# A graph network's edge sweep: edge products in two halves of TensorE, node tiles spread over a block, pass 0's rows through PSUM, and no counting

## The chip, the cores and the metric

The kernel runs on one core of a Trainium2 chip. The metric is the device time of one execution in microseconds (us). Ten executions of the kernel before took 3209.31 to 3219.22 us, with a median of 3214.12 us.

A core has five engines that run their own instruction streams in order and wait for each other by semaphores: TensorE (PE, matrix products, with PEld for its weight loads), VectorE (DVE), ScalarE (ACT), GpSimd (POOL) and SyncE (SP). DMAs are issued from the queues of SP, ACT and POOL. A DMA whose rows are picked by a list of indices (a gather) is issued from POOL, which is busy with it for about a microsecond.

## The reference

The graph has N = 6250 nodes of 256 features and E = 100000 edges, sorted by their target `dst`, with 64 features per edge. There are three message passes:

```
pass 0:  e    = relu((x[dst] - x[src]) @ theta.T + theta_b + x[src] @ phi.T + phi_b)
         out  = segment_max(e, dst), 0 where a node has no edge
         x    = layernorm(x + out)
         hv   = x @ W_in + b_in
pass 1, pass 2 (weights W_u0, then W_u1):
         m    = relu(concat(hv[src], he) @ W + b)
         hv   = hv + segment_max(m, dst) where a node has an edge, else hv
result:  y    = layernorm(x + relu(hv @ W_ro + b_ro))
```

Here `he` are the 64 edge features. All numbers are float32.

## The kernel before

**Tables.** A product with a node's features is the same for all edges that leave it, so each pass has a table in DRAM with one row of 256 numbers per node. An edge's message is its source's table row, plus, in passes 1 and 2, the product of its 64 edge features with the lower part of the weights. Table 0 is made in a prologue; tables 1 and 2 are written tile by tile as node results appear (`first_g` L924 to L928, `next_d` L941 to L944).

**Steps, chunks, blocks.** The edges are laid out in reverse order in 14 blocks. A block has 56 steps (the last 54), FS = 782 in all; step s takes one edge on each of the 128 partitions, and a partition's edges follow each other in a block. Per step GpSimd gathers 128 table rows into `run` (`sources`, L784). Eight steps share one `run` buffer, a chunk; there are four such buffers. The gather for step s + 16 is issued at step s (`AHEAD`). Then VectorE makes the running maximum along each partition: the message of the step before is cut by `lim` (minus a huge number where a new target begins) and compared with the step's row (L1043). Each finished chunk is stored to DRAM as `S` (L1051), on the SP queue. The running value is written over the gathered row, so the first step of a chunk reads the last row of the chunk before.

**Rows of a step.** In pass 0 the row is the gathered one, in SBUF; for 40 of the first 160 steps it is instead made from gathered rows of x (`raw_turn`, `raw_pair`) and lies in PSUM. In passes 1 and 2, `pair` (L816) makes the edge product of two steps at once: the features of the two steps stand one above the other in the 128 rows of the contraction, and the weights `whe` stand twice in a 128 x 512 block with zeros elsewhere. VectorE adds the two gathered rows to it in PSUM (L1030), then does the two steps of the maximum.

**Blocks and nodes.** At the end of a block the running values of the 128 partitions are carried over the lanes (`over_lanes`). The nodes lie in 49 tiles of 128, handled from tile 48 down to tile 0. For a tile, GpSimd gathers from `S` the row where each node's edges end (`rows`, L866, list `end_i`). `picks` and `carried` bring in what was carried from lanes before; then comes the rest of the node's computation, cut into small tasks (`first_a` to `first_g`, `next_a` to `next_d`, `last_d` to `last_g`).

**The order.** It is written out by hand. `at(slot, task)` files a task under a step; the loop over s issues the step's own instructions and then the tasks of that slot. Each engine gets its instructions in this order. A node tile has a base slot b, and a slot g for its gather. In passes 1 and 2 a tile follows the last block that it needs by 20 steps, with a gap of 4 or 6 steps to the tile before. In pass 0 the ends of the nodes' edges must be known first: `count` (L707) makes one-hot matrices from all targets and adds their products on TensorE, three steps apart from step 28 on; `ends_a` and `ends_b` make `has` and `end_i` from the counts. So no tile of pass 0 has a gather before step 324 (`begin`), and tile 48's base is 344.

**From one pass to the next.** The first 24 steps of a pass (`EARLY`) gather only from the part of the table that tiles 1 to 48 wrote. What comes from tile 0 is added on TensorE: a `row` of source numbers is loaded on SP, VectorE makes a 0/1 matrix `own` of it (L824), and TensorE multiplies that with tile 0's result `new0` (L829). Of these 24 gathers, 8 are issued at the last 8 steps of the pass before (`FIRM`) and 16 after the tasks of slot FS:

```
        for f, a in tasks.pop(FS):
            f(*a)
        if r < 2:
            for s in range(FIRM, EARLY):
                sources_next(s)
```

Tile 0 has base FS + 4 = 786 and its gather at slot 782. The later gathers read the whole table and so need tile 0's table write. The edge features of a pass are loaded from ScalarE's queue from the pass's step 0 on (`features`, L811).

Of the kernel before, what the change touches and what calls it, by code (L numbers as in the profile page):

```python
# [17 lines left out]
P = 128  # L18
N = 6250
D = 256  # L20
# [44 lines left out]
WIDE = max(sum(a <= b <= z for a, z in SPAN) for b in range(NB))  # L65

# [7 lines left out]
def gather_raw(nc, x, x_sb, s_r, i):  # L74

    nc.gpsimd.indirect_dma_start(out=x_sb[:, i, :], out_offset=None, in_=x,
                                 in_offset=bass.IndirectOffsetOnAxis(ap=s_r[:, i:i + 1], axis=0))
# [382 lines left out]
def gnn_kernel(  # L460
# [13 lines left out]
    above = const.tile([P, P], F32)  # L474
    nc.vector.tensor_scalar(above, jmp, 0.0, None, OP.is_gt)
# [4 lines left out]
    col = const.tile([P, P], BF16)  # L480
    nc.vector.tensor_copy(col, col_i)
# [30 lines left out]
    lo = const.tile([P, FS], BF16)  # L512
    hi = const.tile([P, FS], BF16)
    with tc.manual_schedule(), tc.tile_pool(name="pro", bufs=2) as pro, \
# [6 lines left out]
        for i in range(SOON):  # L521
            gather_raw(nc, x, x_sb, s_r, i)
        zero = pro.tile([1, D], F32, name="zero", bufs=1)
# [14 lines left out]
        def check():  # L538
# [15 lines left out]
            alike = BLOCKS.count(BLOCKS[0])  # L554
# [9 lines left out]
            nc.vector.tensor_scalar(bits, d_s, P - 1, None, OP.bitwise_and)  # L564
            nc.vector.tensor_copy(lo, bits)
            nc.vector.tensor_scalar(bits, d_s, 7, None, OP.arith_shift_right)
            nc.vector.tensor_copy(hi, bits)
# [29 lines left out]
def in_order(ctx: ExitStack, tc: tile.TileContext, g):  # L597
# [9 lines left out]
    table, ident, above, every, col, col_f = (g[n] for n in ("table", "ident", "above", "every", "col", "col_f"))  # L607
    whole, lim, lo, hi, s_s, fd, pd, ld, nd = (g[n] for n in ("whole", "lim", "lo", "hi", "s_s", "fd", "pd", "ld", "nd"))
    heT, xTn, xn, out = (g[n] for n in ("heT", "xTn", "xn", "out"))
    s_e, head, x, x_sb, wd, s_r = (g[n] for n in ("s_e", "head", "x", "x_sb", "wd", "s_r"))  # L610
    part = g["part"]
# [6 lines left out]
    has = one.tile([P, NT], F32, name="has")  # L618
# [3 lines left out]
    ones = one.tile([P, NT], F32, name="ones")  # L622
    nc.vector.memset(ones, 1.0)
# [30 lines left out]
    for r, w in enumerate((g["w_u0"], g["w_u1"])):  # L654
        t = one.tile([P, 2, D], F32, name=f"whe{r}")
        nc.vector.memset(t, 0.0)
        for s in range(2):
            nc.scalar.dma_start(t[s * DE:(s + 1) * DE, s, :], w[D:, :])
        whe.append(t)
# [36 lines left out]
    hist = psum.tile([P, 512], F32, tag="v", name="hist", bufs=1)  # L696

    none = one.tile([P, NT], BF16, name="none")
    nc.vector.memset(none, 0.0)
    half = (NG + 1) // 2  # L700
    low = []
    for i in range(2):
        low.append(psum.tile([P, 512], F32, tag="he", name="low", bufs=3))
        n = min(half * K, FS - i * half * K)
        nc.scalar.copy(low[i][:, :n], lo[:, i * half * K:i * half * K + n])

    def count(c):  # L707
        k = min(K, FS - c * K)
        ol = work.tile([P, K, P], BF16, name="ol", bufs=1)
        nc.vector.tensor_tensor(ol[:, :k, :], col.unsqueeze(1).to_broadcast([P, k, P]),  # L710
                                low[c // half][:, c % half * K:c % half * K + k].unsqueeze(2).to_broadcast([P, k, P]), OP.is_equal)
        b = max(i for i in range(NB) if FIRST[i] <= c * K)
        tiles = [t for t in range(NT) if SPAN[t][0] <= b <= SPAN[t][1]]
        t0, w = tiles[0], len(tiles)
        oh = work.tile([P, K, WIDE], BF16, name="oh", bufs=1)
        nc.vector.tensor_tensor(oh[:, :k, :w], col[:, t0:t0 + w].unsqueeze(1).to_broadcast([P, k, w]),  # L716
                                hi[:, c * K:c * K + k].unsqueeze(2).to_broadcast([P, k, w]), OP.is_equal)
        if c == 0:
            nc.tensor.matmul(hist[:, :NT], ol[:, 0, :], none, start=True, stop=False)
        for j in range(k):  # L720
            nc.tensor.matmul(hist[:, t0:t0 + w], ol[:, j, :], oh[:, j, :w], start=False,  # L721
                             stop=(c == NG - 1 and j == k - 1))

    cnt, incl, end = (one.tile([P, NT], F32, name=n) for n in ("cnt", "incl", "end"))
    sums = []

    def ends_a():
        nc.vector.tensor_copy(cnt, hist[:, :NT])
        ps = psum.tile([P, 512], F32, tag="pr", name="sums")
        nc.tensor.matmul(ps[:, :NT], above, cnt, start=True, stop=True)  # L730
        nc.tensor.matmul(ps[:, 64:64 + NT], every, cnt, start=True, stop=True)
        sums.append(ps)
        nc.vector.tensor_scalar(has, cnt, 0.0, None, OP.is_gt)

    def ends_b():
        lower, total = sums[0][:, :NT], sums[0][:, 64:64 + NT]
        nc.vector.tensor_tensor_scan(incl, ones, total, 0.0, OP.mult, OP.add)
        nc.vector.tensor_sub(end, total, incl)
        nc.vector.tensor_sub(end, end, lower)
        nc.vector.tensor_add(end, end, has)  # L740
        nc.vector.tensor_scalar(end, end, float(E - 2), 0.0, OP.add, OP.max)
        nc.vector.tensor_copy(end_i, end)
# [14 lines left out]
    def turned(a):  # L757
        tp = psum.tile([P, 512], F32, tag="tp", name="tp")
        for k in range(2):
            nc.tensor.transpose(tp[:, k * P:(k + 1) * P], a[:, k * P:(k + 1) * P], ident)  # L760
        aT = work.tile([P, 2, P], F32, name="aT")
        nc.scalar.copy(aT.rearrange("p k e -> p (k e)"), tp[:, :2 * P])  # L762
        return aT

    def times(aT, w, n, tag="pr"):
        ps = psum.tile([P, 512], F32, tag=tag, name="prod", bufs=3 if tag == "he" else 2)
# [4 lines left out]
    def sweep(r):  # L771
# [7 lines left out]
        carried_in = []  # L779
        pending = []  # L780
# [13 lines left out]
        def raw_turn(i):  # L794

            tp = psum.tile([P, 512], F32, tag="tp", name="tp")
            for q in range(4):
                nc.tensor.transpose(tp[:, q * P:(q + 1) * P], x_sb[:, 2 * i + q // 2, q % 2 * P:(q % 2 + 1) * P], ident)
# [3 lines left out]
        def raw_pair(i):  # L802
            aT = rT.pop(i)
            hp[i * K // 2] = psum.tile([P, 512], F32, tag="pr", name="hp")
            for q in range(4):
                nc.tensor.matmul(hp[i * K // 2][:, q // 2 * D:(q // 2 + 1) * D], aT[:, q, :], wd[:, q % 2, :],
# [9 lines left out]
        def pair(i):  # L816
            c, q = divmod(i, K // 2)
            hp[i] = psum.tile([P, 512], F32, tag="he", name="hp", bufs=3)
            early = 2 * i < EARLY
            if early:  # L820
                row = work.tile([P, 2 * P], I32, name="row")
                nc.sync.dma_start(row, head[i:i + 1, :].to_broadcast([P, 2 * P]))
                own = work.tile([P, 2 * P], F32, name="own")
                nc.vector.tensor_scalar(own, row, part, None, OP.is_equal)  # L824
            nc.tensor.matmul(hp[i], hT[c][:, q, :], whe[r - 1].rearrange("p s f -> p (s f)"), start=True,  # L825
                             stop=not early)
            if early:
# [291 lines left out]
```

## Time and profile before

| what | value |
|---|---|
| median of 10 runs | 3214.12 us |
| profiled execution, its own time | 3213.0 us |
| its span, first to last instruction | 3211.2 us |
| mean granted clock of TensorE | 0.737 |
| HBM read, written | 404.56 MB, 333.17 MB |
| S store, from issue to landing (median) | 4.8 us |
| edge features | 4.4 us |
| table gather | 3.3 us |
| m gather | 2.9 us |
| table write of a tile | 3.6 us |

The profile's page gives for each engine its busy time and share of the span. The costliest groups of instructions show source line, engine, operation, what is written and read, shapes and count; after the bar come the busy time, the mean ns of one, and the engine's idle time just before them with what ended it. "issue" means that the profile shows nothing waited for. In a table by stretches, a row gives the stretch (us from the start), its length, the busy time and number of instructions of the named engine, TensorE's granted clock, the share of time in which DMA engines were busy, and GB/s. A timeline row gives start, duration, engine, line, operation and tiles, how many were merged, and in square brackets the idle time before it and what ended it. An engine's letter with a q (ACTq) is its queue, issuing a DMA.

### The profile page before, as it was taken

How to read it: one execution, taken by the hardware profiler on the slowest of the kernel's cores; microseconds unless marked ns; L12 is line 12 of the kernel's file. 1: busy time of each engine (PE TensorE's matmuls, PEld its weight loads, DVE VectorE, ACT ScalarE, POOL GpSimd, SP SyncE). 2: the span in 40 equal slices, each digit the busy share in tenths (PEclk: the TensorE clock that was granted, in tenths of full speed). 3: DMA queues.
4: the chain of work that ended last, by engine and by line, in shares of the span. 5: the costliest groups of instructions: out<-in, count | busy, mean ns of one | idle time of the engine just before them, and what ended most of it. 6: DMA issues, size and time to landing. Idle time of an engine off the chain costs nothing. (4 is left out here: it accounts for less than half of the span.)

```text
span 3211.2 us, 21650 instructions
## 1 busy us (share of the span) xinstructions
PE 1889.4 (59%) x4631; PEld 849.4 (26%) x4631; DVE 2126.3 (66%) x4750; ACT 238.5 (7%) x618; POOL 2394.6 (75%) x2500
## 2 busy tenths in 40 slices
PE   6663336566511266666666666656666666666665
PEld 5542213222200122232222222223333222222221
DVE  2788756656544376666666666657777777777766
ACT  2000001111100000000000000000001000000000
POOL 6767777777777767777777777776777777777775
PEclk8765556656555588888878877769888888777777
DMA  9769666656666576777667776767767676677775
GB/s 308 242 223 316 220 221 203 206 194 207 206 211 207 194 248 228 233 235 235 228 232 243 236 237 232 235 221 242 241 230 230 233 237 226 234 234 242 236 233 191
DMA packets 241821, 739.39 MB, mean 230 GB/s; under 512 B 52485, under 2 KB 95858, under 8 KB 204434
## 3 DMA queue, kind: packets, MB, share of 16 engines
q0 software_dynamic: 119664, 326.92, 34.1%
q1 hardware_dynamic: 69568, 337.85, 28.3%
q10 hardware_dynamic: 52450, 73.16, 6.8%
q14 instruction: 100, 0.82, 0.1%
q8 instruction: 39, 0.64, 0.1%
HBM read 404.56 MB, written 333.17 MB: 230 GB/s over the span
## 5 line engine op out<-in xcount | busy, mean ns | idle before, releaser
L790 POOL DMA_INDIRECT run<-table,s_s x2258 | 2165.6, 959 | 718.3 <-issue 607.7
L825 PE MATMUL hp<-whe,hT 128*128 128x512 f32 x1564 | 1061.7, 790 | 523.5 <-DVE run L1043 507.3
L1030 DVE TENSOR_TENSOR hp<-hp,run 128x512 f32<-128x512 f32 x782 | 543.8, 695 | 464.1 <-DMA run<-table,s_s 439.3
L1043 DVE SCALAR_TENSOR_TENSOR run<-run,lim,hp 128x256 f32<-128x256 f32 x1573 | 753.7, 479 | 46.8
L825 PEld LDWEIGHTS hp<-whe,hT 128*128 128x128 f32 x1564 | 327.6, 240 | 1079.3 <-DVE run L1043 1021.2
L1043 DVE SCALAR_TENSOR_TENSOR run<-run,lim 128x256 f32<-128x256 f32 x731 | 351.9, 481 | 231.9 <-DMA run<-table,s_s 217.3
L889 PE MATMUL v<-cs,pick 128*128 128x256 f32 (+1 forms) x438 | 167.5, 504 | 140.5 <-DVE pick L882 140.5
L768 PE MATMUL prod<-wcat,aT 128*128 128x512 f32 x196 | 174.6, 1043 | 23.2 <-ACT aT L762 23.2
L870 POOL DMA_INDIRECT m<-S,end_i x147 | 143.5, 976 | 52.7 <-issue 43.2
L889 PEld LDWEIGHTS v<-cs,pick 128*128 128x128 f32 x438 | 104.2, 257 | 253.1 <-issue 147.2
L721 PE MATMUL hist<-oh,ol 128*128 128x8 bf16 (+7 forms) x782 | 34.8, 167 | 177.2 <-DVE oh L716 177.2
L710 DVE TENSOR_TENSOR ol<-col,low 128x1024 bf16<-128x1024 bf16 x98 | 118.7, 1211 | 7.2 <-PE hist L721 7.1
L760 PE MATMUL tp<-ident,h_sb 128*128 128x128 f32 x196 | 49.5, 342 | 120.7 <-DVE h_sb L935 120.2
L932 ACT ACTIVATE m<-m,has 128x256 f32<-128x256 f32 x98 | 49.7, 508 | 697.3 <-DVE m L931 670.1
L840 PE MATMUL lp<-ident,run 128*128 128x128 f32 x84 | 24.9, 393 | 126.0 <-DVE run L1043 117.3
L760 PE MATMUL tp<-ident,x_sb 128*128 128x128 f32 x98 | 31.9, 425 | 110.9 <-DVE x_sb L755 70.8
L768 PE MATMUL prod<-wro,aT 128*128 128x256 f32 x196 | 79.6, 545 | 25.3 <-ACT aT L762 25.3
L721 PEld LDWEIGHTS <-ol 128*128 128x128 bf16 x782 | 36.3, 104 | 202.3 <-DVE ol L710 197.7
L768 PE MATMUL prod<-wt,xT 128*128 128x256 f32 x196 | 88.4, 598 | 0.4 <-DMA xT<-in_xTn 0.4
L762 ACT COPY aT<-tp 128x256 f32<-128x256 f32 x147 | 54.7, 372 | 444.0 <-PE tp L760 421.6
L768 PEld LDWEIGHTS prod<-wcat,aT 128*128 128x128 f32 x196 | 55.9, 313 | 88.7 <-issue 48.1
L760 PEld LDWEIGHTS tp<-ident,h_sb 128*128 128x128 f32 x196 | 23.3, 163 | 210.5 <-issue 123.4
(131 smaller groups left out, 1326.6 us busy)
## 6 DMA issues: line engine op xcount, KB each, us to landing
S<-run SPq DMA_DIRECT2D x291, 1024.0 KB, 4.8
hT<-in_heT ACTq DMA_DIRECT2D x196, 256.0 KB, 4.4
run<-table,s_s POOLq DMA_INDIRECT x2258, 3.3
table<-new ACTq DMA_DIRECT2D x98, 128.0 KB, 3.6
xg<-in_xTn SPq DMA_DIRECT2D x7, 896.0 KB, 9.0
xT<-in_xTn SPq DMA_DIRECT2D x49, 128.0 KB, 5.0
x_sb<-in_xn SPq DMA_DIRECT2D x7, 896.0 KB, 7.5
out<-new ACTq DMA_DIRECT2D x48, 128.0 KB, 2.5
```

The costliest lines, as they stand in the source:

```text
L710: nc.vector.tensor_tensor(ol[:, :k, :], col.unsqueeze(1).to_broadcast([P, k, P]), low[c // half][:, c % half * K:c % half * K + k].unsquee ...
L721: nc.tensor.matmul(hist[:, t0:t0 + w], ol[:, j, :], oh[:, j, :w], start=False, stop=(c == NG - 1 and j == k - 1))
L760: nc.tensor.transpose(tp[:, k * P:(k + 1) * P], a[:, k * P:(k + 1) * P], ident)
L762: nc.scalar.copy(aT.rearrange("p k e -> p (k e)"), tp[:, :2 * P])
L768: nc.tensor.matmul(ps[:, :n], aT[:, k, :], w[:, k, :], start=(k == 0), stop=(k == 1))
L790: nc.gpsimd.indirect_dma_start(out=runs[s // K][:, s % K, :], out_offset=None, in_=table[r][:SPARE + 1, :] if early else table[r], in_offs ...
L825: nc.tensor.matmul(hp[i], hT[c][:, q, :], whe[r - 1].rearrange("p s f -> p (s f)"), start=True, stop=not early)
L870: i = nc.gpsimd.indirect_dma_start(out=o["m"], out_offset=None, in_=S_r[:P * (FIRST[SPAN[t][1]] + BLOCKS[SPAN[t][1]]), :], in_offset=bass. ...
L889: nc.tensor.matmul(o["v"][:, :N1], p, cs[:, blk % KEPT, :N1], start=(blk == SPAN[t][0]), stop=(blk == SPAN[t][1]))
L932: nc.scalar.activation(o["m"], o["m"], AF.Relu, scale=has[:, t:t + 1])
L1030: nc.vector.tensor_add(sums, sums, two)
L1043: nc.vector.scalar_tensor_tensor(cur, prev, lim[:, s:s + 1], row, OP.min, OP.max)
```

## The change

Five things change together.

1. The edge products: `pair` becomes `four`. The 64 features of one step are multiplied with a plain 64 x 256 weight block, in the upper or the lower 64 rows of TensorE according to the step's place, and go to two PSUM tiles, one per half. Four steps are made at once; VectorE's sum covers steps s and s + 2, or s + 1 and s + 3.
2. Pass 0's gathered rows are copied to PSUM by ScalarE, two steps at a time (`bring`), four steps ahead of VectorE, whose maximum then always reads its row from PSUM. The rows from x go into the same PSUM tiles.
3. `count`, `ends_a` and `ends_b` go. A new task `ends` per tile finds where its nodes' edges end by two small masks per block, one product per block with `lane` (each partition's targets, plus one), and two sums on VectorE. `has` becomes `keeps`, a limit of plus or minus a huge number that a minimum applies, so ScalarE's relu with scale in `first_b` and `next_a` is no longer there.
4. Node tiles are spread: the gap is the block's 56 steps divided by its tiles, at least 8; the first base in all three passes is 84, and tile 0's is FS + 6. The theta product stays in PSUM and comes just before its use. The table of x is loaded part by part from step 2 on.
5. PSUM is shared out anew: the tag `he` has four buffers (three before), `tp` one (two before).

The core of the diff:

```diff
+    def ends(t):
+        b0, b1 = SPAN[t]
+        top = work.tile([P, NB], F32, name="top")
+        nc.vector.tensor_scalar(top[:, b0:b1 + 1], fn[:, 0, b0:b1 + 1], float(-P * t), None, OP.add)
+        ps = psum.tile([P, 512], F32, tag="he", name="ends", bufs=4)
+        for b in range(b0, b1 + 1):
+            own = work.tile([P, P], F32, name="here")
+            nc.vector.tensor_scalar(own, col_f, fn[:, 1, b:b + 1], float(-P * t), OP.subtract, OP.is_gt)
+            nc.vector.scalar_tensor_tensor(own, col_f, top[:, b:b + 1], own, OP.is_le, OP.mult)
+            nc.tensor.matmul(ps[:, :BLOCKS[0] + 1], own, lane[:, b, :], start=b == b0, stop=b == b1)
+        found = work.tile([P, 2, BLOCKS[0]], F32, name="found")
+        num = work.tile([P, 2], F32, name="num")
+        for i, op in enumerate((OP.is_ge, OP.is_equal)):
+            nc.vector.scalar_tensor_tensor(found[:, i, :], ps[:, :BLOCKS[0]], n1[:, t:t + 1], every[:, :BLOCKS[0]], op,
+                                           OP.mult, accum_out=num[:, i:i + 1])
+        nc.vector.tensor_scalar(end_i[:, t:t + 1], ps[:, BLOCKS[0]:BLOCKS[0] + 1], num[:, 0:1], 0.0, OP.add, OP.max)
+        nc.vector.tensor_scalar(keeps[:, t:t + 1], num[:, 1:2], 0.0, 2.0 * BIG, OP.is_gt, OP.mult)
+        nc.vector.tensor_scalar(keeps[:, t:t + 1], keeps[:, t:t + 1], -BIG, None, OP.add)
...
+        def bring(i):
+            hp[i] = psum.tile([P, 512], F32, tag="he", name="hp", bufs=4)
+            if raw(2 * i) is None:
+                c, q = divmod(i, K // 2)
+                nc.scalar.copy(hp[i], runs[c][:, 2 * q:2 * q + 2, :].rearrange("p s f -> p (s f)"))
+                return
+            aT = rT.pop(raw(2 * i) // 2)
...
-            nc.tensor.matmul(hp[i], hT[c][:, q, :], whe[r - 1].rearrange("p s f -> p (s f)"), start=True,
-                             stop=not early)
+        def four(u):
+            c, q = divmod(u, K // 4)
+            hp[u] = [psum.tile([P, 512], F32, tag="he", name="hp", bufs=4) for _ in range(2)]
+            early = 4 * u < EARLY
+            n = min(2, FS // 2 - 2 * u)
+            for j in range(n):
+                i = 2 * u + j
+                if early:
+                    row = work.tile([P, 2 * P], I32, name="row")
+                    nc.sync.dma_start(row, head[i:i + 1, :].to_broadcast([P, 2 * P]))
+                    own = work.tile([P, 2 * P], F32, name="own")
+                    nc.vector.tensor_scalar(own, row, part, None, OP.is_equal)
                 for k in range(2):
+                    at_ = slice(k * DE, (k + 1) * DE)
+                    nc.tensor.matmul(hp[u][k][:, j * D:(j + 1) * D], hT[c][at_, 2 * q + j, :], whe[r - 1][at_, :],
+                                     start=True, stop=not early)
+                if early:
+                    for k in range(2):
+                        nc.tensor.matmul(hp[u][k][:, j * D:(j + 1) * D], own[:, k * P:(k + 1) * P], new0, start=False,
+                                         stop=True)
...
-                nc.vector.tensor_add(o["m"], o["m"], h_sb[:, t, :])
-                nc.scalar.activation(o["m"], o["m"], AF.Relu, scale=has[:, t:t + 1])
-
-            def first_c():
-                nc.vector.tensor_add(o["m"], o["m"], x_sb[:, t, :])
+                nc.vector.scalar_tensor_tensor(o["m"], o["m"], keeps[:, t:t + 1], o["h"][:, :D], OP.min, OP.add)
+                nc.vector.scalar_tensor_tensor(o["m"], o["m"], 0.0, x_sb[:, t, :], OP.max, OP.add)
...
-                nc.vector.tensor_max(o["m"], o["m"], o["v"][:, :D])
-                nc.scalar.activation(o["m"], o["m"], AF.Relu, scale=has[:, t:t + 1])
+                nc.vector.scalar_tensor_tensor(o["m"], o["m"], keeps[:, t:t + 1], o["v"][:, :D], OP.min, OP.max)
...
-        gap = (6, 4, 6)[r]
+        last = [FIRST[b] + BLOCKS[b] for _, b in SPAN]
         b = 0
         for t in reversed(range(NT)):
-            e = max(FIRST[SPAN[t][1]] + BLOCKS[SPAN[t][1]], begin)
-            b = max(b + (gap if b < FS else 3), e + 4, min(e + AHEAD + 4, FS + 4))
-            node(t, max(e, b - AHEAD - 4), b)
+            e = last[t]
+            gap = max(8, BLOCKS[0] // last.count(e))
+            b = max(b + gap, e + AHEAD + 12)
+            b = min(b, FS - FIRM - 12 - 8 * (t - 1)) if t else FS + 6
+            node(t, max(min(e + 8, b - 4), b - AHEAD - 4), b)
...
+            if r > 0:
+                if s % 4 == 0 and s + 4 < FS:
+                    four(s // 4 + 1)
+                sums = hp[s // 4][s % 2]
+                if s % 4 < 2:
+                    n = min(2, (FS - s + 1) // 2)
+                    sums = sums.rearrange("p (a f) -> p a f", f=D)[:, :n, :]
+                    nc.vector.tensor_add(sums, sums, runs[c][:, j:j + 2 * n - 1:2, :])
+                row = hp[s // 4][s % 2][:, s % 4 // 2 * D:(s % 4 // 2 + 1) * D]
```

## The prediction

> **What bounds the kernel now.** I read the busy times first, then gather counts by stretch, then the timelines of GpSimd, VectorE, ScalarE and TensorE where one pass hands over to the next.
>
> ```profile
> PE 1889.4 (59%) x4631; PEld 849.4 (26%) x4631; DVE 2126.3 (66%) x4750; ACT 238.5 (7%) x618; POOL 2394.6 (75%) x2500
> ...
> L790 POOL DMA_INDIRECT run<-table,s_s x2258 | 2165.6, 959 | 718.3 <-issue 607.7
> L825 PE MATMUL hp<-whe,hT 128*128 128x512 f32 x1564 | 1061.7, 790 | 523.5 <-DVE run L1043 507.3
> ...
> L1043 DVE SCALAR_TENSOR_TENSOR run<-run,lim 128x256 f32<-128x256 f32 x731 | 351.9, 481 | 231.9 <-DMA run<-table,s_s 217.3
> ```
>
> GpSimd is 75% busy, and nearly all its idle time ends by "issue": 0.30 us between one gather and the next. A gather costs 0.95 + 0.30 = 1.25 us, and there are 2493 of them (2258 + 48 + 147 + 40): 2493 x 1.25 = 3116 of the 3211.2 us. The other engines wait: TensorE idles 523.5 us ahead of its largest group. So only what shortens a gather, or makes GpSimd wait, counts. The number of gathers does not change.
>
> Gathers by stretch (us, GpSimd busy, count):
>
> ```profile
> 80.00:160.00 80.00, 60.49 (x63) 0.75 0.74 244
> 160.00:240.00 80.00, 54.04 (x57) 0.67 0.67 220
> 240.00:480.00 240.00, 183.03 (x188) 0.50 0.76 252
> 480.00:880.00 400.00, 306.72 (x307) 0.62 0.62 204
> 880.00:1090.00 210.00, 159.51 (x165) 0.53 0.61 207
> ...
> 1200.00:2080.00 880.00, 666.15 (x703) 0.81 0.71 234
> 2240.00:3120.00 880.00, 666.27 (x702) 0.80 0.70 235
> ```
>
> Passes 1 and 2 do 1405 gathers in 1760 us, 1.2527 each. Pass 0 does 780 in 1010 us; at 1.2527 that is 977.1, so pass 0 loses 32.9 us. In the timeline of 80 to 240 us, 9.6 us of it are idle gaps above 0.30 (2.76, 2.22, 2.02 and smaller), where VectorE is late while it counts. The other 23.3 are longer gathers (306.72/307 = 1.00 us, against 666.15/703 = 0.948).
>
> GpSimd at the change from pass 0 to 1:
>
> ```profile
> 1096.27 0.95 POOL L790 DMA_INDIRECT run<-table,s_e  x1 [0.30 <-issue]
> 1097.52 0.95 POOL L870 DMA_INDIRECT m<-S,end_i  x1 [0.30 <-issue]
> 1098.78 0.95 POOL L790 DMA_INDIRECT run<-table,s_e  x1 [0.30 <-issue]
> ...
> 1127.56 0.95 POOL L790 DMA_INDIRECT run<-table,s_s  x1 [0.30 <-issue]
> 1135.62 0.94 POOL L790 DMA_INDIRECT run<-table,s_s  x1 [7.11 <-DVE run L1043]
> ```
>
> VectorE over the same stretch, then ScalarE and TensorE:
>
> ```profile
> 1100.33 0.48 DVE L905 SCALAR_TENSOR_TENSOR m<-v,no,m 128x256 f32<-128x256 f32 x1 [5.24 <-DMA m<-S,end_i]
> ...
> 1109.00 0.42 DVE L926 TENSOR_TENSOR new<-prod,b 128x256 f32<-128x256 f32 x1 [5.08 <-PE prod L768]
> ...
> 1120.08 0.69 DVE L1030 TENSOR_TENSOR hp<-hp,run 128x512 f32<-128x512 f32 x1
> ...
> 1133.87 0.35 DVE L824 TENSOR_SCALAR own<-row,part 128x256 f32<-128x256 int32 x1 [6.12 <-DMA row<-in_head]
> ...
> 1134.87 1.00 DVE L1043 SCALAR_TENSOR_TENSOR run<-run,lim,hp 128x256 f32<-128x256 f32 x2
> ```
>
> ```profile
> 1109.85 14.74 ACTq L814 DMA_DIRECT2D hT<-in_heT  x5
> ```
>
> ```profile
> 1115.99 2.07 PE L825 MATMUL hp<-whe,hT 128*128 128x512 f32 x2 [7.03 <-DMA hT<-in_heT]
> ```
>
> This is one chain of 38.1 us. The m gather of node tile 0 (1097.52) lands 2.8 later; the tile is computed (8.7, to 1109.00); ScalarE, in order, only then issues the edge features (0.85), which land (6.1, 1115.99); TensorE makes the first products (4.1, to 1120.08); VectorE does chunk 0 (7.7); the next `row`, queued on SP behind the store of chunk 0, lands, and the first step of chunk 1 runs (7.8): it is the last to read chunk 0's buffer, and GpSimd, four buffers on, has waited 7.11 us for it. Two more waits follow (3.96, 1.60). From pass 1 to 2 the chain is 36.05 us, the waits 5.10, 3.92 and 0.77.
>
> **The change, part by part.**
>
> *Rows of pass 0 through PSUM.* Added: some 371 ScalarE copies of 128x512 x 585 ns (row rT<-tp) = 217 us in a pass of 1010, on an engine 7% busy; they run four steps ahead of VectorE, and what queues behind them (root, turned tile, table write) is late by up to five gathers, 6 us. VectorE's step stays 479 to 481 ns. What goes is the second SBUF operand of 731 steps. In passes 1 and 2 the step reads PSUM, and a gather is 0.948. I take 21 of the 23.3 us, since norms, picks and some 150 new mask operations with SBUF operands stay. Ends: 13 (880 to 1090, hardly any tiles, loses 0.02 a gather: 742 x 0.02, less 2 for the masks) and 24.
>
> [...]
>
> *No counting.* 98 `ol` of 1.21 us, their `oh`, 782 pairs of TensorE and the theta waits go; the 9.6 us of gaps go. In their place, tiles come every 9 steps from step 84 (not every 6 from 344), each with an `ends`: per block a mask (0.29) and its product (0.3), one TensorE answer (about 0.9, as at the scan over lanes), two short reductions, three one-column operations: 2.7 us. VectorE per tile then: 9 steps x 0.52 = 4.65, `ends` 2.7, node 4.2, lanes 0.3: 11.9 us, while GpSimd needs 10 x 1.25 = 12.5. Tight but under; GpSimd runs 16 steps ahead (20 us); less 3.3 for a landing and 4.8 for a store, VectorE may be 12 us late before a row gather waits on the store of its chunk. I charge 2; ends 0 and 12 (one microsecond more per tile, over 17 tiles, less the 5 of slack I trust).
>
> *Products of 64 rows, four steps at a time.* Per two steps, 2 matmul passes of 512 columns become 4 of 256, two in each half: the same time if the halves take turns (0.86 us where a 512 pass takes 0.43, as around 1122; 1.7 where it takes 0.85, as at 1116), less if they overlap, against 2.5 us of gathers. Cover: TensorE's 523.5 idle us. The sum over steps s and s+2 makes VectorE wait for two gathers more, 2.5 us, inside 32 buffered steps: 0. If that cover went, a chunk would wait some 2 us. Single PSUM buffers for turning: 0, behind the same slack. Iotas, fewer memsets, whe without zeros: 0, in the wait for the branch.
>
> *Order at the ends of passes.* Tile 0 moves from step FS+4 to FS+6 and its gather from slot 782 to 784. The rows for the next pass are queued between: in the changed order the m gather now stands behind all 24 early gathers, not behind 8. That is 16 x 1.25 = 20.0 us later, and the chain hangs on it. After it GpSimd must also wait for tile 0's table write (it gathers the whole table), some 15 us, then has 8 gathers, then waits for chunk 0: two waits in place of one, with the same end. Today the 16 gathers fill the chain; after, nothing does. The chain's own length: tile 0 loses the ScalarE relu (-0.5); features on a quieter queue (-0.5); two `own` pairs and four products before the first sum (+1.1: passes of 256 columns at 0.43, later 0.21, make 4.2 to 5.1 us against 3.6, and one `own` more); two `row` and `own` in front of step 8 (+0.7): +0.8. Later waits: +0.8 and -1.3. Per change of pass 20.3 to 20.8, twice: +41. Ends: 32 (hT and `row` land 6 sooner in sum: shortest rows 2.8 and 2.9, against 6.1 and 5.6, some of it lost again) and 46. The table write of tile 1, now at step 771, may hold the first early gather: +0.5 (0 to 3).
>
> [...]
>
> *Tail.* The last two steps' sums are single, the relu of tile 0 goes: -1 (0 to -1.5).
>
> Sum: -21 - 9.6 + 2 + 41 + 0.5 - 1 = +12 on the profiled execution's own 3213.0 us, which is 1.1 under the median of 3214.1: **3225 us**.
>
> **The rivals.**
>
> *Faster: a short chain.* If, with GpSimd silent after tile 0, every landing in the chain shrinks (features, `row`, store), the later m gather costs less. With the other terms at -29 it breaks even at 15 us per change of pass, and decides for faster by 0.2% at 12. For it: features landed in 2.8 us at 1151.74. Against it: the 20 us are a queue position, the arithmetic of the chain (some 23 of 38 us: 8.7, 0.85, 4.1, 7.7 and the last step) stays. At 10 per change: 3204.
>
> *Pass 0 becomes VectorE's.* 11.9 of 12.5 us leaves nothing for waits on TensorE's answers or on ScalarE behind its copies. In 160 to 240 us VectorE was 82% busy and GpSimd still lost 9 us. If each of the first 17 tiles takes 1 us over, +10: 3235.
>
> *The gathers stay long.* If it is not the second SBUF operand, or ScalarE's reads disturb as well, the -21 goes: 3246. Against it: the groups with and without `hp` differ in nothing else.
>
> **How the numbers follow.** The forecast's case, 3221 to 3237: 0.56. Near-cancellation (chains 3 to 8 us shorter each, or all 24 us of long gathers gone), 3208 to 3220: 0.20. Short chain: 0.14. Pass 0 VectorE's: 0.07. Gathers stay long: 0.03. A measurement here tells about 0.2%, 6.4 us, from no change, so slower is 0.56 + 0.07 + 0.03 = 0.66, same 0.20, faster 0.14. The range leaves out the short chain and the long gathers: from 3213 + 32 - 24 - 9.6 - 1.5 = 3210 to 3213 + 46 - 13 - 9.6 + 6 + 1 = 3243, taken as 3209 to 3243.
>
> **What would show it.** Right: gathers of pass 0 at 0.95 us; no gaps around 160 to 240; the m gather of tile 0 behind 24 early ones, and after it waits of about 14 and 13 us at both changes of pass; TensorE less busy and not missed. Wrong: a wait after the m gather under 10 us in all, pass 0 gathers at 0.98, or gaps in the first 300 us.

## The result and the profile after

The changed kernel takes 3227.68 us (median of 8 runs, 3225.77 to 3231.57). The kernel before takes 3213.42 us (median of 28 runs). The ratio is 1.0046, with a 95% interval of 1.0037 to 1.0055. The forecast was 3225 us, and "slower by over 0.2%" was its likeliest case.

Eight runs below, marked "disturbed", fell in sessions in which every kernel, the one before too, took 3990 to 4283 us with transfers at 173 to 183 GB/s (229 to 234 in the other traces), and in which all versions of the changed order took 4.9 to 5.5% longer than the kernel before for a cause that no run looks for, so that their times tell nothing of the 14 us.

The busy times and the costliest groups in the page of the changed kernel:

```profile
PE 1793.3 (56%) x5554; PEld 1075.8 (33%) x5554; DVE 2109.7 (65%) x5083; ACT 370.6 (11%) x840; POOL 2365.4 (73%) x2503
...
L767 POOL DMA_INDIRECT run<-table,s_s x2258 | 2140.7, 948 | 752.2 <-issue 624.2
L1032 DVE SCALAR_TENSOR_TENSOR run<-run,lim,hp 128x256 f32<-128x256 f32 x2304 | 1102.4, 478 | 204.1 <-ACT hp L784 133.7
L813 PE MATMUL hp<-whe,hT 64*128 64x256 f32 x3128 | 855.2, 615 | 377.4 <-DVE run L1032 362.9
...
L784 ACT COPY hp<-run 128x512 f32<-128x512 f32 x371 | 218.4, 590 | 584.8 <-DMA run<-table,s_s 476.9
```

GpSimd was busy 2394.6 us and is now busy 2365.4 us, with the same 2493 gathers: 29.2 us less. Yet the span grew from 3211.2 to 3228.3 us. So GpSimd stands idle some 46 us more than before. The question of this case is where.

GpSimd's gathers by stretch of the changed kernel (us, busy time and count, granted clock, DMA share, GB/s):

```profile
80.00:160.00 80.00, 60.50 (x64) 0.73 0.85 299
160.00:240.00 80.00, 53.08 (x56) 0.85 0.69 230
240.00:480.00 240.00, 181.62 (x192) 0.68 0.68 225
480.00:880.00 400.00, 302.71 (x320) 0.61 0.65 216
880.00:1060.00 180.00, 136.14 (x145) 0.52 0.63 212
1200.00:2080.00 880.00, 665.85 (x704) 0.59 0.70 235
```

In 480 to 880 us there were 307 gathers before and there are 320 now, at 302.71/320 = 0.946 us, the same as in pass 1 (665.85/704 = 0.946). Pass 0 has lost its long gathers. GpSimd over the whole of pass 0, kernel before and then changed kernel:

```profile
4.00:1087.30 1083.30, 816.11 (x830) 0.61 0.68 228
```

```profile
4.00:1062.20 1058.20, 788.19 (x833) 0.65 0.69 232
```

So 27.9 of the 29.2 us lie in pass 0. Only the stretch 160 to 240 us still does not keep the pace: 56 gathers in 80 us, where 64 fit.

GpSimd at the change from pass 0 to pass 1, changed kernel (start, duration, in brackets the idle time before and what ended it):

```profile
1091.21 0.95 POOL L767 DMA_INDIRECT run<-table,s_e  x1 [0.30 <-issue]
1092.46 0.95 POOL L859 DMA_INDIRECT m<-S,end_i  x1 [0.30 <-issue]
1108.75 0.94 POOL L767 DMA_INDIRECT run<-table,s_s  x1 [15.35 <-issue]
...
1131.49 0.94 POOL L767 DMA_INDIRECT run<-table,s_s  x1 [13.04 <-DVE run L1032]
...
1146.12 0.94 POOL L767 DMA_INDIRECT run<-table,s_s  x1 [4.93 <-DVE run L1032]
```

Tile 0's gather of m (1092.46) now comes after the last early gather (`s_e`). Nothing is left to do beside the chain that hangs on it. GpSimd waits 15.35 us for tile 0's table write (the row names nothing; at the next change the trace names the write), then 13.04 us for the first step of chunk 1, then 4.93 and 1.46 us. That is 34.8 us where the kernel before lost 12.7 (7.11, 3.96, 1.60). At the change from pass 1 to 2 the waits are 9.21, 14.82, 6.24, 0.57 and 1.47 us, 32.3 in all, where they were 10.4.

The other place is the crowded stretch of pass 0. First GpSimd, then SP's queue, then VectorE in the changed kernel:

```profile
205.30 0.94 POOL L859 DMA_INDIRECT m<-S,end_i  x1 [7.78 <-DVE sd L730]
...
216.57 0.99 POOL L859 DMA_INDIRECT m<-S,end_i  x1 [2.84 <-DVE sd L730]
```

```profile
200.34 0.32 SPq L1040 DMA_DIRECT2D S<-run  x1
...
211.02 6.98 SPq L1040 DMA_DIRECT2D S<-run  x2
```

```profile
198.53 0.28 DVE L714 SCALAR_TENSOR_TENSOR found<-ends,n,every 128x56 f32<-128x56 f32 x1 [3.53 <-PE ends L710]
```

Two gathers of m stand 7.78 and 2.84 us, 10.0 more than the usual 0.30 each. (In the other undisturbed traces of the changed order the two waits add up to between 7.1 and 12.7 us.) The name in the brackets (`sd`) is only VectorE's last instruction before. What they wait for is in SP's queue: the stores of their chunks are issued at 200.34 and 211.02, some 5 us before each gather starts, and such a store lands 4.7 us after its issue (median of the page). The stores are late because VectorE is late, and one of the things it stands for, by the trace, is the product `ends` of the new end search.

### The profile page after: what moved, and what is told of

It is laid out like the page before. It is cut to its first block, busy times and chain, and to the rows that moved or that the text cites. A ratio compares the mean times of both kernels' runs of the same rounds, so it can differ in the third digit from the quotient of the medians.

```text
span 3228.3 us, 24669 instructions
## 1 busy us (share of the span) xinstructions
PE 1793.3 (56%) x5554; PEld 1075.8 (33%) x5554; DVE 2109.7 (65%) x5083; ACT 370.6 (11%) x840; POOL 2365.4 (73%) x2503
## 3 DMA queue, kind: packets, MB, share of 16 engines
q1 hardware_dynamic: 69568, 337.85, 27.9%
## 5 line engine op out<-in xcount | busy, mean ns | idle before, releaser
L767 POOL DMA_INDIRECT run<-table,s_s x2258 | 2140.7, 948 | 752.2 <-issue 624.2
L1032 DVE SCALAR_TENSOR_TENSOR run<-run,lim,hp 128x256 f32<-128x256 f32 x2304 | 1102.4, 478 | 204.1 <-ACT hp L784 133.7
L813 PE MATMUL hp<-whe,hT 64*128 64x256 f32 x3128 | 855.2, 615 | 377.4 <-DVE run L1032 362.9
L1016 DVE TENSOR_TENSOR hp<-hp,run 128x512 f32<-128x512 f32 (+1 forms) x784 | 544.2, 694 | 488.1 <-DMA run<-table,s_s 382.0
L813 PEld LDWEIGHTS hp<-whe,hT 64*128 64x128 f32 x3128 | 531.8, 294 | 677.7 <-DVE run L1032 533.5
L784 ACT COPY hp<-run 128x512 f32<-128x512 f32 x371 | 218.4, 590 | 584.8 <-DMA run<-table,s_s 476.9
L878 PE MATMUL v<-cs,pick 128*128 128x256 f32 (+1 forms) x438 | 197.0, 577 | 131.6 <-DVE pick L871 131.6
L744 PE MATMUL prod<-wu,aT 128*128 128x256 f32 x196 | 97.3, 648 | 22.7 <-ACT aT L738 22.7
L744 PEld LDWEIGHTS prod<-wt,xT 128*128 128x128 f32 x196 | 53.5, 284 | 66.2 <-issue 25.7
L726 ACT ACTIVATE sd<-mv,eps 128x1 f32<-128x1 f32 x98 | 28.8, 294 | 402.5 <-DVE mv L724 402.3
```

Source lines behind the costliest of these rows:

```text
L726: nc.scalar.activation(sd, mv[:, 1:2], AF.Sqrt, bias=eps)
L744: nc.tensor.matmul(ps[:, :n], aT[:, k, :], w[:, k, :], start=(k == 0), stop=(k == 1))
L767: nc.gpsimd.indirect_dma_start(out=runs[s // K][:, s % K, :], out_offset=None, in_=table[r][:SPARE + 1, :] if early else table[r], in_offs ...
L784: nc.scalar.copy(hp[i], runs[c][:, 2 * q:2 * q + 2, :].rearrange("p s f -> p (s f)"))
L813: nc.tensor.matmul(hp[u][k][:, j * D:(j + 1) * D], hT[c][at_, 2 * q + j, :], whe[r - 1][at_, :], start=True, stop=not early)
L878: nc.tensor.matmul(o["v"][:, :N1], p, cs[:, blk % KEPT, :N1], start=(blk == SPAN[t][0]), stop=(blk == SPAN[t][1]))
```

## The experiments

**Tile 0's gather of m back among the early gathers, in the changed kernel.**

```
-            node(t, max(min(e + 8, b - 4), b - AHEAD - 4), b)
+            node(t, max(min(e + 8, b - 4), b - AHEAD - 4) if t else FS, b)
```

> The changed kernel, with one thing put back: tile 0's m gather goes to slot FS, ahead of the 16 early gathers, in all three passes. Theory (queue position): the gather is 16 x 1.25 = 20 us sooner at each change of pass, the waits after it fall from 34.8 and 31.7 us to 12 to 15 each, and the time to 3188 us (3182 to 3194). Rival (the waits come from the new products and their order, not from the place in the queue): the waits move with the gather and stay above 25 us each, the time stays above 3215.

Disturbed: 4269.48 us, the kernel before 4059.41. The same file again:

> The changed kernel with tile 0's m gather at slot FS again, ahead of the 16 early gathers, as in the run before of the same kernel, which met transfers that stood still for 10 to 20 us in both kernels. Where the kernel before takes its 3213 us: theory (queue position) 3188 us (3182 to 3194), waits after the gather of 12 to 15 us at each change of pass; rival (the waits come from the new products and their order) above 3215 and waits above 25 us. Where transfers stand still again, the chip decides and nothing of this can be read.

Measured: 3188.38 us (3187.15 to 3191.94), the kernel before 3213.96; ratio 0.9917 (0.9901 to 0.9934). One moved instruction is worth 3227.7 - 3188.4 = 39.3 us, and with it the change as a whole is a gain of 25.6 us. GpSimd in this run at the same change of pass:

```profile
1071.46 0.95 POOL L767 DMA_INDIRECT run<-table,s_e  x1 [0.31 <-issue]
1072.71 0.95 POOL L859 DMA_INDIRECT m<-S,end_i  x1 [0.30 <-issue]
1073.96 0.95 POOL L767 DMA_INDIRECT run<-table,s_e  x1 [0.30 <-issue]
...
1112.22 0.94 POOL L767 DMA_INDIRECT run<-table,s_s  x1 [8.57 <-DVE run L1032]
...
1128.19 0.94 POOL L767 DMA_INDIRECT run<-table,s_s  x1 [6.28 <-DVE run L1032]
```

The gather starts 19.75 us earlier (1072.71 against 1092.46), 16 early gathers run beside the chain, the wait for the table write is gone, and the wait for chunk 1 is 8.57 us again (7.11 before the change). The waits add up to 16.1 us here and 12.5 us at the next change, against 34.8 and 32.3: 38.5 us less, which is the time gained. (The expectation had 12 to 15 us at each change.) This settles the largest term.

**The same move alone, on the kernel before.** Tile 0's gather behind all the early ones.

```
-            node(t, max(e, b - AHEAD - 4), b)
+            node(t, max(e, b - AHEAD - 4) if t else FS + 2, b)
```

> The kernel before, with one thing from the change: tile 0's m gather goes to slot FS + 2, behind the 16 early gathers, in all three passes. Theory (queue position): waits at the two changes of pass grow by some 20 us each, time 3213 + 40 = 3253 us (3247 to 3259). Rival (the old kernel's chain had room, or a silent GpSimd makes the landings short): under 3225.

> The kernel before with one number changed: tile 0's gather of m issued at slot FS + 2 of the pass, behind all 24 early gathers, where the changed kernel has it. Theory, that this place alone makes what the changed kernel loses at the changes of pass (22.1 and 22 us by the idle time of GpSimd; 39.3 us came off when the changed kernel got it back): 3213 + 32 to 46, so 3245 to 3259 us. Rival, that it needs the crowded VectorE of the changed kernel beside it: 3218 to 3235 us.

Both sessions were disturbed: 1.0024 (0.9998 to 1.005) and 1.0032 (1.0006 to 1.0059), 1.5 and 12 us on some 4050. Neither the theory nor its rival is tested, since in such a session the gain of 39 us from moving it back does not show either (4269.48 us with it, 4246.65 us for the changed kernel with only the end search moved, below). Whether the place alone costs 40 us in the kernel before stays unmeasured.

**Pass 0's rows from SBUF again.** The changed kernel without ScalarE's copies; all else stays.

```
-            hp[i] = psum.tile([P, 512], F32, tag="he", name="hp", bufs=4)
+            if raw(2 * i) is not None:
+                hp[i] = psum.tile([P, 512], F32, tag="he", name="hp", bufs=4)
...
-                nc.scalar.copy(hp[i], runs[c][:, 2 * q:2 * q + 2, :].rearrange("p s f -> p (s f)"))
+                hp[i] = runs[c][:, 2 * q:2 * q + 2, :].rearrange("p s f -> p (s f)")
```

> The changed kernel without ScalarE's copies: pass 0's gathered rows stay in SBUF and the maximum reads them there; the rows made from x still lie in PSUM. Theory (the second SBUF operand lengthens the gathers): pass 0's gathers are 0.975 to 1.00 us again, +20 to +30 us, time 3248 to 3258. Rival (the counting or the crowded tiles made them long): gathers stay at 0.95, time 3222 to 3230, or less if ScalarE's copies had held anything up.

> The changed kernel without ScalarE's copies in pass 0 (the maximum reads the gathered rows in SBUF), where transfers run as in the run on record. Theory (the second SBUF operand lengthens the gathers): pass 0's gathers 0.975 to 1.00 us again, +20 to +30 us against the changed kernel's 3227.7, time 3248 to 3258. Rival (the counting or the crowded tiles made them long): gathers stay at 0.95, time 3222 to 3230, or less if ScalarE's copies had held anything up.

> The changed kernel without ScalarE's copies: pass 0's rows are added from SBUF as before the change. Theory, that the second operand in SBUF is what makes gathers of pass 0 longer (0.97 us where they are 0.946, some 770 gathers): 15 to 24 us more than the changed kernel, 3243 to 3253 us. Rival, that the length goes with VectorE's load or with ScalarE, which is idle now: gathers at 0.946 us still, and 3222 to 3232 us.

All three sessions were disturbed (4271.62, 4210.53 and 4271.08 us), so the times decide nothing. The length of one gather can still be compared inside such sessions. GpSimd's groups in 100 to 1250 us, with tile 0's gather moved and the copies in (first fence), and without the copies (two sessions):

```profile
L767 POOL DMA_INDIRECT run<-table,s_s x638 | 604.5, 947 | 279.1 <-issue 187.7 <-DMA S<-run 23.9 <-ACT hp L784 18.2
```

```profile
L767 POOL DMA_INDIRECT run<-table,s_s x670 | 647.3, 966 | 269.3 <-issue 191.9 <-DVE run L1033 41.9 <-DMA S<-run 11.3
```

```profile
L767 POOL DMA_INDIRECT run<-table,s_s x651 | 630.3, 968 | 280.3 <-issue 192.2 <-DVE run L1033 28.4 <-DMA S<-run 24.0
```

The mean goes from 947 to 966 and 968 ns (972 in the third session), with VectorE 47 to 49% busy in all four. In passes 1 and 2 of the same traces, where the edit changes nothing, it is 947 to 949 with and without the copies. So the second SBUF operand of VectorE's step does lengthen the gathers, by some 0.02 us each, a little less than the expected 0.975 us and more; the rival (VectorE's load, or ScalarE) falls. On 780 gathers that is 15 to 20 us. In such sessions the kernel before has 976 and 977 ns there, so the rows account for two thirds or more of the difference; the rest comes from other parts of the change and is not assigned.

**The end search two slots later.**

```
-                slot = g - 12
+                slot = g - 10
```

> The changed kernel, the task ends two slots later (10 steps ahead of the tile's gather, not 12). Theory (VectorE stands still because ends' small product queues on TensorE behind another tile's turn and 512-wide product, 2.4 to 6.6 us instead of 1): the two waits of 7.8 and 2.8 us near 205 and 217 us shrink or go, time 3217 to 3223. Rival (VectorE is simply full there, 11.9 of 12.5 us): the waits stay within 2 us of what they are, time 3226 to 3230.

> The changed kernel with one number changed: the first tiles' count product `ends` is issued at the tenth task before its gather instead of the twelfth, so that VectorE's turn for `found` comes later and TensorE has had time for it. Theory, that the 7.8 and 2.8 us that gathers of m wait around 205 and 217 us come from VectorE standing for `ends` behind other tiles' products: some 4 to 10 us go, 3218 to 3224 us. Rival, that VectorE is simply full there: 3226 to 3231 us, with the same waits. Rival of the other sign, that two tasks less are too few for the indices: 3232 us or more.

The first session was disturbed (4246.65 us). The second: 3231.25 us (3226.78 to 3235.62), ratio 1.0046 (1.0032 to 1.006), the same as the changed kernel and not the 3218 to 3224 of the theory. What GpSimd waited for in 190 to 225 us, and VectorE in 110 to 205 us, in this run (the name behind the arrow is the last releaser that the profile has):

```profile
POOL m L859 <- DVE m L894: 9.3, 1, 9.3
...
POOL m L859 <- DVE m L898: 3.1, 1, 3.1
```

```profile
DVE found L714 <- PE ends L710: 18.1, 8, 4.5
```

The same VectorE row of the changed kernel:

```profile
DVE found L714 <- PE ends L710: 16.4, 8, 6.6
```

The columns are the sum, the count and the longest. The edit did not take the wait for `ends` away: 18.1 us against 16.4 in eight waits. It moves the product and VectorE's use of it together, so the distance between them stayed. That these waits make the gathers of m late is therefore argued from the trace and not shown by a run; that two slots of delay don't help is shown. Nor is the rival shown, that VectorE is simply full there, though its time (3226 to 3231 us) and its waits are the ones that came.

**Products in full height.** The changed kernel with its weights padded with zeros to 128 rows, so that the products don't use the halves; the count of products stays.

```
-        t = one.tile([P, D], F32, name=f"whe{r}")
+        t = one.tile([P, 2, D], F32, name=f"whe{r}")
+        nc.vector.memset(t, 0.0)
...
-                    nc.tensor.matmul(hp[u][k][:, j * D:(j + 1) * D], hT[c][at_, 2 * q + j, :], whe[r - 1][at_, :],
+                    nc.tensor.matmul(hp[u][k][:, j * D:(j + 1) * D], hT[c][:, 2 * q + j, :], whe[r - 1][:, k, :],
```

> The changed kernel with the edge products in full height again, the weight padded with zeros (one product of 128 rows per step, the same count of them), so that two steps no longer run in the two halves of TensorE. Theory, that TensorE is off the chain that sets the end and the halves are worth nothing in time: 3224 to 3231 us, the products some 250 to 450 ns where they are 615 and waiting less for each other, and the granted clock back above 0.68 from 0.61 if it is the halves that lower it. Rival, that TensorE's turns set the pace of the crowded tiles: a time some 5 us or more away from 3228.

Measured: 3226.0 us (3224.85 to 3228.84), against 3227.68 with the halves: no difference that can be told. The first products of pass 1 on TensorE, changed kernel, then full height:

```profile
1109.93 1.23 PE L813 MATMUL hp<-whe,hT 64*128 64x256 f32 x4 [6.73 <-DMA hT<-in_heT]
1111.08 2.07 PE L817 MATMUL hp<-new,own 128*128 128x256 f32 x4
1113.09 1.23 PE L813 MATMUL hp<-whe,hT 64*128 64x256 f32 x4
```

```profile
1105.08 2.08 PE L813 MATMUL hp<-whe,hT 128*128 128x256 f32 x4 [6.78 <-DMA hT<-in_heT]
1106.94 1.60 PE L817 MATMUL hp<-new,own 128*128 128x256 f32 x4
1108.38 1.03 PE L813 MATMUL hp<-whe,hT 128*128 128x256 f32 x4
```

Four products take 1.23 us in the halves and 2.08 us in full height, both at a granted clock of 0.50; of those in the halves the first two, one in each half, take 0.80 us together, where each takes 0.79, so the halves do run side by side. The first sum on VectorE starts 6.69 us after the first product in the halves (1116.62) and 5.50 us after it in full height (1110.58). The granted clock has a part in that: in full height four products take 2.08 us at 0.50 (1105.08) and 1.03 us at 1.00 (1109.24). TensorE in the halves, then in full height (us, busy, count, granted clock, DMA share, GB/s):

```profile
1109.00:1116.00 7.00, 6.07 (x16) 0.50 0.58 183
1117.00:1122.00 5.00, 5.00 (x25) 1.00 0.48 142
```

```profile
1105.00:1108.00 3.00, 2.92 (x7) 0.50 0.51 177
1109.00:1117.00 8.00, 8.00 (x38) 1.00 0.48 150
```

The clock is 1.00 from 3.0 us after the first product on in full height, and only from 6.5 us after it in the halves. At the change from pass 1 to 2 it is the other way round: the first sum comes 6.01 us after the first product in the halves (2180.24 to 2186.25) and 6.43 us after it in full height (2174.99 to 2181.42), with the clock at 1.00 after 4.5 and 4.9 us. GpSimd's waits at the two changes add up to 34.8 and 32.3 us in the halves, and to 35.1 and 32.3 us in full height. So at the changes of pass the halves neither cost nor bring anything that lasts.

TensorE in passes 1 and 2, full height and then halves (us, busy, count, granted clock, DMA share, GB/s):

```profile
1200.00:2080.00 880.00, 553.42 (x1790) 0.81 0.70 235
2260.00:3140.00 880.00, 564.03 (x1784) 0.80 0.70 234
```

```profile
1200.00:2080.00 880.00, 549.91 (x1780) 0.59 0.70 235
2260.00:3140.00 880.00, 552.32 (x1780) 0.60 0.70 234
```

**Everything that the chain waits for, issued earlier.** From the run with tile 0's gather moved, two landings are still on the chain: the edge features (`hT`) for TensorE's first product, and `row` for chunk 1. Here the loads of both are issued before the 16 early gathers, and the end search is two slots later as above.

```
+        def load(i):
+            lines[i] = work.tile([P, 2 * P], I32, name="row", bufs=5)
+            nc.sync.dma_start(lines[i], head[i:i + 1, :].to_broadcast([P, 2 * P]))
...
-                    nc.vector.tensor_scalar(own, row, part, None, OP.is_equal)
+                    nc.vector.tensor_scalar(own, lines.pop(i), part, None, OP.is_equal)
+                    if i + 4 < EARLY // 2:
+                        load(i + 4)
...
-            node(t, max(min(e + 8, b - 4), b - AHEAD - 4), b)
+            node(t, max(min(e + 8, b - 4), b - AHEAD - 4) if t else FS, b)
...
-        hT, hp, rT = {}, {}, {}
+        hT, hp, rT = soon.pop(r, {}), {}, {}
...
         if r < 2:
+            hT = soon.setdefault(r + 1, {})
+            for i in range(4):
+                features(i)
+            for i in range(4):
+                load(i)
             for s in range(FIRM, EARLY):
                 sources_next(s)
```

> The changed kernel with tile 0's gather of m at the first slot of the pass (3188.4 us by itself), the count's matmul of `ends` issued two tasks later, the first transposes of the next pass's features issued ahead of the 16 early gathers, and the loads of `row` for these gathers issued four ahead. Theory: what is left at each change of pass in the run with tile 0's gather moved is 8.6 + 6.3 + 1.2 us and 4.8 + 6.0 + 0.6 + 1.2 us; the first of each pair is a wait behind work that could be issued sooner, so some 6 to 12 us go over both changes, and some 5 to 10 of the 12.8 us that wait for `ends` around 205 and 217 us: 3165 to 3180 us. Rival, that these waits only change their place since the chain of tile 0 (39.7 us) stays as long as it is: 3185 to 3190 us. Rival of the other sign, that the work put earlier stands in VectorE's queue ahead of the gathers' indices: above 3195 us.

Disturbed: 4209.46 us, the kernel before 3999.82.

> The same kernel as the run before, on another chip: on the first chip every kernel, the one before the change too, took some 800 us longer, so that its time says nothing of the waits that are asked after. Theory: 3165 to 3180 us (the waits that were left at the changes of pass in the run with tile 0's gather moved, 16.1 and 12.5 us, lose 6 to 12 us together, and of the 12.8 us that wait for `ends` around 205 and 217 us 5 to 10 go). Rival, that the chain of tile 0 holds them where they are: 3185 to 3190 us. Rival of the other sign, that the work put earlier stands in VectorE's queue ahead of the gathers' indices: above 3195 us.

Measured: 3168.49 us (3167.64 to 3172.2), the kernel before 3216.49; ratio 0.9858 (0.9841 to 0.9874). This version beats both kernels. TensorE where pass 1 begins, first with only tile 0's gather moved, then in this run:

```profile
1090.83 1.22 PE L813 MATMUL hp<-whe,hT 64*128 64x256 f32 x4 [7.00 <-DMA hT<-in_heT]
...
1110.26 2.08 PE L817 MATMUL hp<-new,own 128*128 128x256 f32 x4 [4.97 <-DVE own L810]
```

```profile
1086.03 0.86 PE L817 MATMUL hp<-whe,hT 64*128 64x256 f32 x4
1087.09 1.13 PE L821 MATMUL hp<-new,own 128*128 128x256 f32 x4 [0.20 <-DVE own L812]
```

The 7.00 us for the features and the later 4.97 us behind `row` are gone, and TensorE, with no pause since tile 0's own products, takes 1.13 us for four 128-row products from 1087 on, as it does in the changed kernel at a granted clock of 1.00 (1116.94 us there). GpSimd in this run:

```profile
1073.48 0.94 POOL L863 DMA_INDIRECT m<-S,end_i  x1 [1.71 <-DMA S<-run]
...
1104.71 0.95 POOL L767 DMA_INDIRECT run<-table,s_s  x1 [0.30 <-DVE run L1034]
```

The chain (39.5 us with only tile 0's gather moved, 1072.71 to 1112.22, which the expectation has as 39.7) is down to at most 31.2 us and no longer makes GpSimd wait. Of the waits of 16.1 and 12.5 us only 1.71 and 1.82 us are left, both ahead of the gathers of m; the trace names a store of `S` for the first. The sum came out inside the expected 3165 to 3180, but by other shares than expected: the changes of pass gave some 25 us, not 6 to 12, and the waits of the crowded stretch (7.55 and 4.17 us here) nothing. What features and `row` are worth one by one was not tried.

## Why the prediction was right

**The sum, term by term.** The idle time of GpSimd and the length of its gathers explain the difference of the two spans, 17.1 us: -29.2 (gathers) - 9.6 (the gaps of the count) + 10.0 (crowded stretch) + 22.1 + 21.9 (changes of pass) - 0.2 (tail) + 2.9 (a wait in the prologue, 6.92 us against 4.05) = +17.9. The wait in the prologue is between 3.6 and 4.8 us in the other undisturbed runs of the changed order, so it is chance; the profiled execution, at 3230.23 us, is 2.6 us above the median.

**Order at the ends of passes, +41: right.** Measured +44.0 by the idle times, and 39.3 by moving the gather back. The two waits that the prediction named "about 14 and 13" are 15.35 and 13.04 at the first change, 9.21 and 14.82 at the second. Its reason, that the 16 gathers which filled the chain are now ahead of it, is what the run with the gather moved back shows. The chain's own length was put at +0.8. At the first change it grew from 38.1 (1097.52 to 1135.62) to 39.0 us (1092.46 to 1131.49), at the second it shrank from 36.1 to 34.7. Inside it one item was off: from the first product to the first sum it takes 6.69 and 6.01 us where 4.2 to 5.1 was the estimate. The estimate went over to the short products too soon: the granted clock is 0.50 for the first 6.5 and 4.5 us.

The first chunk alternates products of 64 and of 128 rows, and in the changed kernel's trace a group behind such a change takes longer. At a granted clock of 0.50 a group of four 128-row products there takes 2.01 us to the next group (1111.08 to 1113.09), where four at the 0.427 us from start to start inside a group take 1.7. At a clock of 1.00 it takes 1.06 us (1116.94 to 1118.00), where in full height it takes 0.86 (1108.38 to 1109.24). At 0.3 and 0.2 us a change, the eight changes of the first chunk come to some 2 us, an estimate; in the time of the whole kernel it does not show (3227.68 us, and 3226.0 in full height). What the 0.3 and 0.2 us are spent on, no run shows.

**Rows of pass 0 through PSUM, -21: right in kind, too small.** Pass 0 does its 777 gathers between 80 and 1060 us at 734.05/777 = 0.945 us, so none of their extra length is left; the prediction kept back 2 us for operations with SBUF operands that turned out to cost nothing visible. And there was more to lose than the 23.3 us that it counted: GpSimd's busy time in pass 0 fell by 27.9 us (816.11 to 788.19), above the upper end of 24 that it set. In passes 1 and 2 it fell by 1.3 us together. By the runs without the copies 15 to 20 us of this are VectorE's second SBUF operand.

That is 0.02 us a gather with rows in SBUF (947 ns to 966 and 968), where a step of VectorE lasts 0.48. In what way the step lengthens the gather, no run shows.

**No counting, -9.6 and +2: the first right, the second mis-sized.** The gaps of the count are gone. The crowded stretch costs 10.0 us and not 2; the step that failed is the price of "one TensorE answer (about 0.9, as at the scan over lanes)". VectorE waits 16.4 us for eight answers in 110 to 205 us, 2.05 each, and in the trace the small product `ends` stands in TensorE's queue behind a tile's larger ones:

```profile
193.35 2.61 PE L788 MATMUL hp<-wd,rT 128*128 128x256 f32 x8
195.80 1.88 PE L744 MATMUL prod<-wcat,aT 128*128 128x512 f32 x4
...
197.95 0.55 PE L710 MATMUL ends<-lane,here 128*128 128x57 f32 x4
```

That is the "one microsecond more per tile" from which the prediction made the upper end of 12. It also counted VectorE's load tile by tile and found it "tight but under", which left no room for a wait of one microsecond. That this wait makes the 10.0 us is read from the trace; the run with the end search two slots later did not take it away and so doesn't test it.

**Products of 64 rows, 0: right**, by the run in full height (3226.0 against 3227.7). **Tail, -1:** -0.2; **tile 1's table write, +0.5:** 0, the first early gather at 1062.46 us waits 0.30.

**The rivals.** The short chain (breaking even at 15 us per change) is out: 22 us were lost at each change, and the chain grew by 0.9 us at one and shrank by 1.4 at the other. Gathers that stay long are out: 0.946. Pass 0 becoming VectorE's is half true: 10 us, and that case was priced at exactly +10, but for the first 17 tiles and not for two waits.

So the total was met within 3 us while two terms were each off by some 8 us, in opposite directions (gathers 29.2 for 21, crowded stretch 10.0 for 2). That they cancelled is luck; the sign rested on the term that was right. The upper end of the range, 3243, counts 6 us for the crowded stretch and 1 for the table write, where the prediction's own ends for them are 12 and 3; with these it would be 3251.

## What to carry to other kernels

Where one engine's queue sets the pace, work out at each change of stage what stands behind what in that queue: here 16 independent gathers issued ahead of one dependent gather cost 39 us, more than the 25.6 us that the change gains without them, and the cure was one slot number. Then look for the loads that the dependent chain waits for and can't use sooner than they are asked for; issuing the features and index rows before the filler work brought another 20 us (in a run that also moved the end search, which alone brought nothing). A small product that another engine waits for can cost its place in the queue more than its own length: by the trace, VectorE waited 3.53 us for four `ends` products of 0.55 us.

## What was not expected of the hardware

- A group of four edge products takes 1.23 us in the halves of TensorE and 2.08 us in full height (granted clock 0.50 in both), but the granted clock in passes 1 and 2 falls from 0.81 and 0.80 to 0.59 and 0.60, and TensorE's busy time there stays about the same (549.91 against 553.42 us in pass 1). With the weights padded with zeros the clock is 0.81 and 0.80 again. The mean over the execution is 0.737 before the change, 0.614 after it, and 0.751 in full height.
- Where the first products of passes 1 and 2 start in the changed kernel, 6.73 and 6.70 us after TensorE's last ones, its granted clock is 0.50, and products take longer than later at 1.00 (four of 128 rows: 2.07 us at 1111.08, 1.13 at 1116.94). From the first product to the clock of 1.00 it took 3.0 and 4.9 us at the two changes of pass in full height, and 6.5 and 4.5 us where halves and full height alternate. What sets the moment is not shown, nor that the pause lowers the clock: at the second change it was 0.50 already at tile 0's products ahead of the pause (2171.4 to 2173.6 us). In the last run, with no pause between tile 0's products and the first ones of the pass, four 128-row products take 1.13 us from the second group on, the time that goes with 1.00 in the changed kernel.
